# Merged stores and paired reads in a five-stage macaron block, with half-precision projections and fewer token buffers

## The chip, the cores and the metric

The kernel runs on one core of a Trainium2 chip. The metric is device time in microseconds (us) of one execution, and a kernel's figure is the median of several executions. Profile views come from one further execution that was profiled.

Engine names: PE is TensorE (PEld its weight loads), DVE is VectorE, ACT is ScalarE, POOL is GpSimd, SP is SyncE, which here only issues transfers. A trailing q (SPq, ACTq) means the sequencer of that engine, for instance while it issues a DMA. L134 is line 134 of the kernel.

## The reference

The input is `x` of 8 sequences by 1024 tokens by 256 channels. Three residual blocks follow one another:

```python
x = x + 0.5 * ffn(layernorm(x))
x = x + attn(layernorm(x))
x = x + 0.5 * ffn(layernorm(x))        # the same weights as the first

def ffn(x):                            # x_prev: the token before, zero at the start
    xr = mu_r * x + (1 - mu_r) * x_prev
    xk = mu_k * x + (1 - mu_k) * x_prev
    return sigmoid(xr @ W_r.T) * (square(relu(xk @ W_k.T)) @ W_v.T)

def attn(x):                           # 16 heads of 16; 40 offsets o: 0..32, 48, 64, 96, 128, 192, 256, 384
    q, k, v = split(x @ qkv_w.T + qkv_b)
    logit[o] = (q[n] . k[n-o]) / 4 * (1 + q[n] . scale_embed[o]) + pos_bias[o]   # masked where n < o
    out = sum_o softmax(logit)[o] * v[n-o] * if_gain
    return (out * sigmoid(x @ gate_w.T + gate_b)) @ out_w.T + out_b
```

Every query therefore looks at 33 near keys ("local") and 7 far ones.

## The kernel before

A *chunk* is 256 tokens (32 of them), a *tile* is 128 tokens (64 of them), a *half* is 512 tokens of a sequence (16 of them, index `i`; `hf` says first or second half). Five generators each do their part of the work step by step:

- `stage_f1`, the first FFN, one chunk per step. Its `load` reads a chunk into `x1[c]` (L220), from a pool `px1` of 13 buffers. A buffer lives until `stage_f2` has stored the chunk (L229).
- `stage_p`, the projections, one chunk per step. The normalised and transposed input is split into `xh` and the remainder `xl`, both float32r, and the weights likewise into `wa_hi` and `wa_lo`. `proj` sums three products (high by high, high by low, low by high), 12 matmuls for each of q, k and the gate, and 12 more for v. For q and for k, and for each half `g` of the channels, ACT writes the float16 value and DVE the float16 remainder into a tile `hl` (L263, L264, four buffers). Two transfers then write that tile to DRAM in two arrangements (L270), since q is needed as high, low, high, low and k as high, high, low, low.
- `stage_qk`, the scores, four steps per half. It reads q (`qst`, L317) and k (`kb`, L319) back from DRAM, and computes far scores and then local scores of 128 queries at a time. `scores` fills a PSUM bank per `g`, ACT copies it into a tile `sl` (L308, two buffers), and four transfers of 32 partitions each store the tile: far scores at L346, local scores at L362. In the first half of a sequence there are two tiles of far scores, in the second half four; local scores always take four tiles.
- `stage_att`, the attention, one tile per step. It loads the tile's local scores along the diagonals (`lg`, L377, three buffers), the far scores (`ef`, L379, two buffers), the local values (`vw`, L385, two transfers into one of two tiles) and the values at distance 32, 48 and 64 (`v3`, L391, L395). Scaling by `1 + q.scale_embed` is L405 and L410, the softmax L419 to L430. The local probabilities are stored (L426, on ACT's queue) and read back into `pd` (L428, one buffer) so that PE can transpose them (L464) and multiply them with `vw` (L473). Every second tile the output projection is added to `x1` (L505).
- `stage_f2`, the second FFN, one chunk per step, and the store of the result.

`norm_transposed` writes two tiles `xn` (L160) per chunk, which PE transposes into one PSUM bank (L162). The stages run in lanes: `stage_f1` has the lane "a", `stage_f2` mostly "b", `stage_p` mostly "p", and each lane has its own PSUM bank (tag `"ps" + s`) and its own two `xn` buffers (tag `"xn" + s`).

The order of the work is fixed at compile time. The steps are sorted by their place plus an offset from `TRACE`; each runs under a priority of its place plus an offset from `RANK`, and the framework's scheduler, which has a timing model, turns the priorities into one order per engine. Each engine, and the queue of each issuing engine, executes that order strictly.

```python
TRACE = (0, 3.6, -4.4, -8.1, -10.6)      # att, f2, qk, p, f1
RANK = (0, 5.1, -4.4, -8.1, -10.6)
for k, kind, stage in sorted(steps, key=lambda s: (s[0] + TRACE[s[1]], s[1])):
    with tc.high_priority(-int(1000 * (k + RANK[kind] + 20))):
        next(stage)
```

`k` counts tiles. Other pools that bound how far a stage may run ahead are `pga` (five gates), `pvn` (six chunks of values) and `pq` (four q tiles).

Of the kernel before, what the change touches and what calls it, by code (L numbers as in the profile page):

```python
# [8 lines left out]
F32 = mybir.dt.float32  # L9
F32R = mybir.dt.float32r  # L10
# [29 lines left out]
F2A = 28  # L40
TRACE = (0, 3.6, -4.4, -8.1, -10.6)
# [8 lines left out]
def macaron(ctx: ExitStack, tc: tile.TileContext, x, wffn, watt, wo, cols, rows, pbias, se, mask, out):  # L50
# [16 lines left out]
    wa_hi = const.tile([128, 4, 2, 256], F32R, name="wa_hi")  # L67
    wa_lo = const.tile([128, 4, 2, 256], F32R, name="wa_lo")
# [4 lines left out]
    vw = [const.tile([128, 4, 2, 8, 17], F32, name=f"vw{i}") for i in range(2)]  # L73
# [7 lines left out]
    px1 = pool("px1", 13)  # L81
# [11 lines left out]
    def load_att():  # L93
        with tc.tile_pool(name="setup", bufs=1) as sp:
            wst = sp.tile([128, 4, 2, 256], F32, name="wst")
            nc.sync.dma_start(wst, watt.rearrange("w (c p) d -> p w c d", p=128))
            nc.vector.tensor_scalar(wst[:, 0], wst[:, 0], 0.25, None, ALU.mult)
            nc.vector.tensor_copy(wa_hi, wst)
            nc.vector.tensor_tensor(wa_lo, wst, wa_hi.bitcast(F32), ALU.subtract)
            nc.vector.tensor_scalar(b_q, b_q, 0.25, None, ALU.mult)  # L100
            nc.vector.tensor_scalar(b_g, b_g, 0.5, None, ALU.mult)
            nc.sync.dma_start(row, rows.unsqueeze(0).to_broadcast([128, 2, 256]))
            for t in [t.bitcast(F32) for t in kb] + vw:
                nc.gpsimd.memset(t, 0.0)
            zero = kb[1].bitcast(F32).rearrange("p a b w -> p (a b w)")
            for i in range(2):
                nc.sync.dma_start(v_d[i][0 : VPAD * VROW].rearrange("(p w) -> p w", p=VPAD), zero[:VPAD, :VROW])
            nc.sync.dma_start(sf_d[0:PADF].rearrange("(p w) -> p w", p=16), zero[:16, : PADF // 16])
            for c0, c1, w in ((0, 8, 384), (8, 15, 384), (15, 16, 368)):
                o = PADF + c0 * ROW + ROW - 384  # L110
                nc.sync.dma_start(flat(sf_d, o, (SF_T, 32), (ROW, c1 - c0), (1, w)), zero[:32, : (c1 - c0) * w])
            nc.sync.dma_start(flat(pd_d, NL * 16, (4 * SKEW, 128), (SKEW, 4), (1, SKEW - NL * 16)), zero[:, : 4 * 512])
            nc.sync.dma_start(bias, pbias.to_broadcast([128, NO * 16]))
            nc.sync.dma_start(msk, mask.rearrange("t p u -> p t u"))
            nc.sync.dma_start(wot, wo.rearrange("(c p) d -> p c d", p=128))
            for c in range(2):
                nc.vector.tensor_scalar(wot[:, c], wot[:, c], gain[:, c : c + 1], 0.5, ALU.mult, ALU.mult)
            se_f = sp.tile([128, NO], F32, name="se_f")
            se_h = sp.tile([128, NO], F16, name="se_h")
            for h2 in range(2):  # L120
                nc.sync.dma_start(se_f[64 * h2 : 64 * h2 + 64], se.unsqueeze(1).to_broadcast([16, 4, NO]))
            nc.vector.memset(seb, 0.0)
            nc.vector.tensor_scalar(se_f, se_f, 4.0, None, ALU.mult)
            nc.vector.tensor_copy(se_h, se_f)
            nc.vector.tensor_tensor(se_f, se_f, se_h, ALU.subtract)
            nc.vector.tensor_scalar(se_f, se_f, slot[:, 1:2], None, ALU.mult)
            for h2 in range(2):
                a = slice(64 * h2, 64 * h2 + 64)
                nc.vector.scalar_tensor_tensor(seb[a, h2], se_h[a], slot[a, 0:1], se_f[a], ALU.mult, ALU.add)
# [25 lines left out]
    def norm_transposed(x2, y, nb, k0, s):  # L155
        tr = ps.tile([128, 2, 256], F32, name="tr", tag="ps" + s)
        for i in range(2):
            k = k0 + i
            xn = pw.tile([128, 256], F32, name="xn", tag="xn" + s, bufs=2)
            nc.scalar.activation(xn, x2[:, i], AF.Identity, bias=nb[:, k : k + 1], scale=y[:, k : k + 1])  # L160
            for c in range(2):
                nc.tensor.transpose(tr[:, c, i * 128 : i * 128 + 128], xn[:, c * 128 : c * 128 + 128], ident)  # L162
        return tr
# [69 lines left out]
    def stage_p():  # L233
        for c in range(NCH):
# [7 lines left out]
            xh = pw.tile([128, 2, 256], F32R, name="xh", tag="xk" + s)  # L242
            xl = pw.tile([128, 2, 256], F32R, name="xl", tag="xr" + s)
            nc.scalar.copy(xh, tr)
            nc.vector.tensor_tensor(xl, tr, xh.bitcast(F32), ALU.subtract)
# [13 lines left out]
            for j, bb in ((0, b_q), (1, b_k)):  # L259
                p = proj(j)  # L260
                for g in range(2):
                    hl = pw.tile([128, 2, 256], F16, name="hl", bufs=4)
                    nc.scalar.activation(hl[:, 0], p[:, g], AF.Identity, bias=bb[:, g : g + 1])  # L263
                    nc.vector.scalar_tensor_tensor(  # L264
                        hl[:, 1], p[:, g], bb[:, g : g + 1], hl[:, 0], ALU.add, ALU.subtract
                    )
                    o = g * 128 * 2048 + cq * 256
                    for r in range(2):
                        ro, s2 = (r * 1024, 512) if j == 0 else (r * 512, 1024)
                        nc.sync.dma_start(flat(qk_d[i % 2][j], o + ro, (2048, 128), (s2, 2), (1, 256)), hl)  # L270
            p = proj(3)
            for g in range(2):
                nc.scalar.activation(gt[:, g], p[:, g], AF.Tanh, bias=b_g[:, g : g + 1], scale=0.5)
# [23 lines left out]
    def stage_qk():  # L297
        def scores(o, g, q4, q, k, keys):
# [9 lines left out]
            nc.scalar.copy(o[:, :, :, g], p.rearrange("n (q h j) -> n j h q", q=4, h=2))  # L308

        for i in range(2 * B):  # L310
# [14 lines left out]
            for th in range(nth):  # L325
                sf = psb.tile([128, 64, 2, 2, 4], F32, name="sl")
                for g in range(2):
                    scores(
                        sf,
                        g,  # L330
                        lambda a: [slice(c, 512, 16) for c in range((4 * th + a) * ns, (4 * th + a + 1) * ns)],
                        qs[i, g],
                        kb[g],
                        lambda ms: slice(LW + ms.start, LW + (hf + 1) * 512, 16),
                    )
                for a in range(4):
                    c = (4 * th + a) * ns
                    o = PADF + hf * 32 * SF_T + c * ROW
                    src = sf[32 * a : 32 * a + 32].rearrange("n j h g q -> n (j h g q)")
                    if hf == 0:  # L340
                        dst = flat(far, o, (SF_T, 32), (ROW, 2), (1, 512))
                        src = src.rearrange("n (s w) -> n s w", s=2)
                    else:
                        w = ROW - 16 if c == 15 else ROW
                        dst, src = flat(far, o, (SF_T, 32), (1, w)), src[:, :w]
                    nc.sync.dma_start(dst, src)  # L346
                if 2 * th + 2 == nth:
                    yield
            yield
            for t in range(4):  # L350
                sl = psb.tile([128, 64, 2, 2, 4], F32, name="sl")
                for g in range(2):
                    scores(
                        sl,
# [5 lines left out]
                    )  # L360
                for a in range(4):
                    nc.sync.dma_start(  # L362
                        flat(sl_d[i % 2], (4 * t + a) * BLK, (ROW, 32), (1, ROW)),
                        sl[32 * a : 32 * a + 32].rearrange("n j h g q -> n (j h g q)"),
                    )
                if t % 2:
                    yield

    def stage_att():
        for tt in range(B * NT):  # L370
# [3 lines left out]
            lg = pat.tile([128, NO, 16], F32, name="lg", bufs=3)  # L374
            ll = lg[:, 0:NL].rearrange("p u e -> p (u e)")
            lf = lg[:, NL:]
            nc.sync.dma_start(ll, flat(sl_d[i % 2], 4 * t4 * BLK, (SKEW, 128), (1, NL * 16)))  # L377
            ef = pat.tile([128, FW, 16], F32, name="ef")
            nc.sync.dma_start(  # L379
                ef.rearrange("p u e -> p (u e)"),  # L380
                flat(sf_d, PADF - 384 + t * 128 * ROW, (ROW, 128), (1, FW * 16)),
            )
            vwt = vw[tt % 2]
            for h2 in range(2):
                nc.sync.dma_start(  # L385
                    vwt[h2::2, :, h2].rearrange("p q a w -> p q (a w)"),
                    flat(v_d[b % 2], (VPAD - LW + t * 128) * VROW + h2 * 136, (VROW, 64), (32 * VROW, 4), (1, 136)),
                )
            v3 = v3s[tt] = pv1.tile([128, 3, 16, 17], F32, name="v3")
# [7 lines left out]
            )  # L397
            for h2 in range(2):
                gp = ps.tile([128, 64, 8], F32, name="gp")
                for g in range(2):  # L400
# [5 lines left out]
                    lg[:, 0:NL, e], gp[:, 0:NL], 1.0, lg[:, 0:NL, e], ALU.add, ALU.mult  # L406
                )
                for k0, k1 in FARG:
# [4 lines left out]
                        1.0,  # L413
# [172 lines left out]
```

## Time and profile before

| what | us |
|---|---|
| median of 3 executions | 1260.52 (1255.84 to 1267.22) |
| the profiled execution | 1256.76 |
| its span, first to last instruction | 1254.0 |
| PE busy | 1089.2 (87%) |
| DVE busy | 942.6 (75%) |
| POOL busy | 766.5 (61%) |
| ACT busy | 538.0 (43%) |

The granted TensorE clock was 0.956 of full speed. DMA moved 282.88 MB. Busy time counts each engine's own instructions as a union of their spans; for PE it includes the pipelined ends of matmuls, so it is more than the array's own time. The *chain of waits* is the chain of work that ended last, followed back from the last instruction to whatever released each step. A group row gives line, engine, operation, tiles written and read, shapes, count, then busy us and mean ns, then idle time before the group and what ended it. A row of DMA issues gives KB per transfer and the median us from issue to landing.

### The profile page before, as it was taken

The page shows a single profiled execution, that of the slowest core. Times are in us where ns is not written, and L with a number is a line of the kernel's source. Part 1 is how long each engine was busy: PE and PEld are TensorE (multiplying, and loading weights), DVE is VectorE, ACT ScalarE, POOL GpSimd, SP SyncE. Part 2 cuts the span into 40 slices and gives each one's busy share as a digit, 9 for nine tenths or more (in the row PEclk, how much of TensorE's full clock was granted, in tenths as well). Part 3 has the DMA queues.
Part 4 walks back from the last instruction along what each step waited for, and adds up shares of the span by engine and source line. Part 5 has one row for each costly group of instructions (what it writes and reads, how often), then busy time and mean ns, then how long its engine had stood idle before and what let it go on. Part 6 is the DMA issues. An engine that isn't in the chain of part 4 may idle for free.

```text
span 1254.0 us, 34712 instructions
## 1 busy us (share of the span) xinstructions
PE 1089.2 (87%) x13568; PEld 885.7 (71%) x13568; DVE 942.6 (75%) x2266; ACT 538.0 (43%) x1025; POOL 766.5 (61%) x1101
## 2 busy tenths in 40 slices
PE   2887989899799898989899989899988998888785
PEld 2676768677687677777777778786777787665664
DVE  7546768987587888879678866978858887877772
ACT  2444445344453444536345454544534444524231
POOL 7436619675575656659457564867656755657672
PEclk9999999899999999899999999999989999998988
DMA  8187888786878779787788977797787868998630
GB/s 263 32 224 222 241 242 265 229 238 194 251 226 254 230 233 274 221 252 232 193 260 257 254 201 230 228 269 227 233 243 234 269 197 254 284 280 265 202 99 24
DMA packets 256500, 282.88 MB, mean 226 GB/s; under 512 B 23440, under 2 KB 214608, under 8 KB 256336
## 3 DMA queue, kind: packets, MB, share of 16 engines
q1 hardware_dynamic: 247120, 263.36, 71.7%
q10 hardware_dynamic: 9216, 17.31, 3.8%
q8 instruction: 106, 1.74, 0.6%
q14 instruction: 58, 0.48, 0.1%
HBM read 151.67 MB, written 128.91 MB: 224 GB/s over the span
## 4 chain that ended last, share of the span: by engine, by line
PE 42%; DMA 25%; DVE 14%; SPq 6%; POOL 5%; issue 5%; ACT 4%; POOLq 0%; ACTq 0%; DVEq 0%
PE p L134 29%; DMA pd<-pd 9%; PE tra L464 4%; PE pv L134 3%; PE tra L134 3%; POOL prod L445 2%; DMA lg<-sl 2%; DMA x<-in_x_dram 2%; DMA qk<-hl 2%; DMA kb<-qk 2%; DMA sl<-sl 2%; DVE prod L457 2%; DVE xk L196 1%; PE gp L134 1%; DVE mx L423 1%
## 5 line engine op out<-in xcount | busy, mean ns | idle before, releaser
L134 PEld LDWEIGHTS <-qst 128*32 128x32 f16 (+1 forms) x5120 | 157.2, 120 | 100.1 <-issue 63.5
L134 PE MATMUL p<-kb,qst 128*32 128x128 f16 (+1 forms) x4096 | 185.1, 297 | 12.7 <-ACT sl L308 8.6
L308 ACT COPY sl<-p 128x512 f32<-128x512 f32 x224 | 130.8, 584 | 144.2 <-PE p L134 123.0
L445 POOL TENSOR_TENSOR prod<-v,lg 128x256 f32<-128x256 f32 x248 | 165.5, 687 | 10.2 <-ACT lg L425 6.1
L134 PE MATMUL p<-xk,w_f 128*128 128x256 f32 x512 | 144.9, 421 | 20.0 <-DVE xk L196 11.7
L419 POOL TENSOR_TENSOR lg<-lg,bias 128x640 f32<-128x640 f32 x64 | 113.5, 1774 | 71.8 <-DVE lg L410 66.9
L213 POOL TENSOR_TENSOR x<-x,xr 128x512 f32<-128x512 f32 x64 | 88.4, 1382 | 109.0 <-DVE xr L212 94.9
L457 DVE TENSOR_TENSOR prod<-prod 128x512 f32<-128x512 f32 (+2 forms) x120 | 126.1, 1051 | 32.1 <-POOL prod L445 31.5
L464 PE MATMUL tra<-ident,pd 128*128 128x128 f32 x512 | 97.1, 313 | 58.3 <-DMA pd<-pd 54.9
L160 ACT ACTIVATE xn<-x,nb,y 128x256 f32<-128x256 f32 x192 | 110.8, 602 | 63.0 <-DVE nb L152 55.2
L134 PE MATMUL p<-w_f,xk 128*128 128x256 f32 x512 | 132.9, 400 | 1.7 <-ACT xr L206 1.3
L134 PE MATMUL p<-w_f,xr 128*128 128x256 f32 x512 | 130.4, 396 | 3.6 <-ACT xk L201 2.8
L445 POOL TENSOR_TENSOR prod<-vn,lg 128x256 f32<-128x256 f32 x144 | 96.0, 678 | 54.3 <-ACT lg L425 35.4
L134 PE MATMUL p<-xh,wa_hi 128*128 128x256 f32 x384 | 123.2, 321 | 5.6 <-DVE hl L264 4.4
L134 PEld LDWEIGHTS p<-xk,w_f 128*128 128x128 f32 x512 | 99.3, 208 | 39.8 <-issue 10.5
L470 ACT COPY ptt<-tra 128x512 f32<-128x512 f32 x128 | 74.9, 585 | 116.1 <-PE tra L464 113.0
L464 PEld LDWEIGHTS tra<-ident,pd 128*128 128x128 f32 x512 | 71.0, 197 | 73.9 <-DMA pd<-pd 68.0
L263 ACT ACTIVATE hl<-p,col 128x256 f16<-128x256 f32 x128 | 60.6, 474 | 121.1 <-PE p L134 68.6
L134 PE MATMUL p<-xh,wa_lo 128*128 128x256 f32 x384 | 111.5, 290 | 0.0
L134 PE MATMUL p<-xl,wa_hi 128*128 128x256 f32 x384 | 111.4, 290 | 0.0
L134 PEld LDWEIGHTS p<-w_f,xr 128*128 128x128 f32 x512 | 95.3, 196 | 19.4 <-ACT xk L201 5.8
L134 PEld LDWEIGHTS p<-w_f,xk 128*128 128x128 f32 x512 | 96.0, 198 | 15.9 <-issue 2.8
(82 smaller groups left out, 2394.2 us busy)
## 6 DMA issues: line engine op xcount, KB each, us to landing
qk<-hl SPq DMA_DIRECT2D x256, 128.0 KB, 3.4
sl<-sl SPq DMA_DIRECT2D x256, 128.0 KB, 3.8
pd<-pd SPq DMA_DIRECT2D x64, 512.0 KB, 4.8
sf<-sl SPq DMA_DIRECT2D x184, 128.0 KB, 3.1
vw<-vd SPq DMA_DIRECT2D x128, 136.0 KB, 4.1
v<-vd SPq DMA_DIRECT2D x64, 272.0 KB, 4.3
lg<-sl SPq DMA_DIRECT2D x64, 264.0 KB, 4.1
pd<-lg ACTq DMA_DIRECT2D x64, 264.0 KB, 3.8
```

What stands on the lines that cost most here:

```text
L134: nc.tensor.matmul(o, l, r, start=start, stop=stop)
L160: nc.scalar.activation(xn, x2[:, i], AF.Identity, bias=nb[:, k : k + 1], scale=y[:, k : k + 1])
L196: nc.vector.scalar_tensor_tensor(o[:, h], xr[:, h], mu[:, h : h + 1], prev[:, h], ALU.mult, ALU.add)
L213: nc.gpsimd.tensor_tensor(x2, x2, xr, ALU.add)
L263: nc.scalar.activation(hl[:, 0], p[:, g], AF.Identity, bias=bb[:, g : g + 1])
L308: nc.scalar.copy(o[:, :, :, g], p.rearrange("n (q h j) -> n j h q", q=4, h=2))
L419: nc.gpsimd.tensor_tensor(la, la, bias, ALU.add)
L423: nc.vector.tensor_reduce(mx, lg.rearrange("p u e -> p e u"), AX.X, ALU.max)
L445: nc.gpsimd.tensor_tensor(prod[:, k], shifted[k][1]()[:, :, 0:16], lf[:, k].unsqueeze(2).to_broadcast([128, 16, 16]), ALU.mult,)
L457: nc.vector.tensor_tensor(o, terms[:, 0:m], terms[:, n - m : n], ALU.add)
L464: nc.tensor.transpose(tr[:, pr * 128 : pr * 128 + 128], pd.rearrange("p (m e) -> p m e", e=8)[:, :, 4 * g + pr], ident,)
L470: nc.scalar.copy(ptt.rearrange("p q n -> p (q n)"), tr)
```

## The change

1. The projections use float16 for `xh`, `xl`, `wa_hi` and `wa_lo` instead of float32r. Weights and biases are scaled by 16 (`WS`), and later operations take the factor out again.
2. `hl` is `[128, 2, 2, 256]`: ACT and DVE read the PSUM result through a broadcast and write it twice, in the arrangement that DRAM wants, and one transfer stores it. There are two such buffers instead of four.
3. `sl` holds two tiles of scores (still two buffers), and each group of 32 partitions is stored once for both. In the first half of a sequence both far tiles fall into one step and the next step is empty.
4. `lg`, `ef` and `vw` hold two tiles; they are read at every even tile. `lg` has two buffers of two tiles instead of three of one, `ef` one of two tiles instead of two of one, `vw` two of two tiles instead of two of one.
5. `px1` has 10 buffers instead of 13, and all lanes share three `xn` buffers instead of having two each.

```diff
-    wa_hi = const.tile([128, 4, 2, 256], F32R, name="wa_hi")
-    wa_lo = const.tile([128, 4, 2, 256], F32R, name="wa_lo")
+    wa_hi = const.tile([128, 4, 2, 256], F16, name="wa_hi")
+    wa_lo = const.tile([128, 4, 2, 256], F16, name="wa_lo")
...
-    vw = [const.tile([128, 4, 2, 8, 17], F32, name=f"vw{i}") for i in range(2)]
+    vw = [const.tile([128, 8, 2, 8, 17], F32, name=f"vw{i}") for i in range(2)]
...
-    px1 = pool("px1", 13)
+    px1 = pool("px1", 10)
...
-            xn = pw.tile([128, 256], F32, name="xn", tag="xn" + s, bufs=2)
+            xn = pw.tile([128, 256], F32, name="xn", bufs=3)
...
-            xh = pw.tile([128, 2, 256], F32R, name="xh", tag="xk" + s)
-            xl = pw.tile([128, 2, 256], F32R, name="xl", tag="xr" + s)
+            xh = pw.tile([128, 2, 256], F16, name="xh", tag="xh" + s)
+            xl = pw.tile([128, 2, 256], F16, name="xl", tag="xl" + s)
...
-                    hl = pw.tile([128, 2, 256], F16, name="hl", bufs=4)
-                    nc.scalar.activation(hl[:, 0], p[:, g], AF.Identity, bias=bb[:, g : g + 1])
-                    nc.vector.scalar_tensor_tensor(
-                        hl[:, 1], p[:, g], bb[:, g : g + 1], hl[:, 0], ALU.add, ALU.subtract
-                    )
-                    o = g * 128 * 2048 + cq * 256
-                    for r in range(2):
-                        ro, s2 = (r * 1024, 512) if j == 0 else (r * 512, 1024)
-                        nc.sync.dma_start(flat(qk_d[i % 2][j], o + ro, (2048, 128), (s2, 2), (1, 256)), hl)
+                    hl = pw.tile([128, 2, 2, 256], F16, name="hl", bufs=2)
+                    hi, lo = (hl[:, :, 0], hl[:, :, 1]) if j == 0 else (hl[:, 0], hl[:, 1])
+                    pp = p[:, g : g + 1].to_broadcast([128, 2, 256])
+                    nc.scalar.activation(hi, pp, AF.Identity, bias=bb[:, g : g + 1])
+                    nc.vector.scalar_tensor_tensor(lo, pp, bb[:, g : g + 1], hi, ALU.add, ALU.subtract)
+                    nc.sync.dma_start(
+                        flat(qk_d[i % 2][j], g * 128 * 2048 + cq * 256, (2048, 128), (512, 4), (1, 256)),
+                        hl.rearrange("p a b n -> p (a b) n"),
+                    )
...
-                sf = psb.tile([128, 64, 2, 2, 4], F32, name="sl")
+                if th % 2 == 0:
+                    sf = psb.tile([128, 2, 64, 2, 2, 4], F32, name="sl")
...
+                if th % 2 == 0:
+                    continue
...
-                if 2 * th + 2 == nth:
+                if hf and th == 1:
                     yield
+            if not hf:
+                yield
             yield
...
-                    nc.sync.dma_start(
-                        flat(sl_d[i % 2], (4 * t + a) * BLK, (ROW, 32), (1, ROW)),
-                        sl[32 * a : 32 * a + 32].rearrange("n j h g q -> n (j h g q)"),
-                    )
+                        flat(sl_d[i % 2], (4 * (t - 1) + a) * BLK, (ROW, 32), (4 * BLK, 2), (1, ROW)),
+                        sl[32 * a : 32 * a + 32].rearrange("n t j h g q -> n t (j h g q)"),
+                    )
...
-            lg = pat.tile([128, NO, 16], F32, name="lg", bufs=3)
...
-            ef = pat.tile([128, FW, 16], F32, name="ef")
...
-            vwt = vw[tt % 2]
...
+            if j == 0:
+                lg2 = pat.tile([128, 2, NO, 16], F32, name="lg")
...
+                ef2 = pat.tile([128, 2, FW, 16], F32, name="ef", bufs=1)
...
+                vw2 = vw[tt // 2 % 2]
...
+            lg, ef, vwt = lg2[:, j], ef2[:, j], vw2[:, 4 * j : 4 * j + 4]
```

## The prediction

> **What bounds the kernel now.** I read busy shares first, then the chain of waits, then the SP queue's own waits, then the timeline of the matmuls that change type.
>
> ```profile
> PE 1089.2 (87%) x13568; PEld 885.7 (71%) x13568; DVE 942.6 (75%) x2266; ACT 538.0 (43%) x1025; POOL 766.5 (61%) x1101
> ...
> DMA  8187888786878779787788977797787868998630
> ...
> q1 hardware_dynamic: 247120, 263.36, 71.7%
> ...
> PE 42%; DMA 25%; DVE 14%; SPq 6%; POOL 5%; issue 5%; ACT 4%; POOLq 0%; ACTq 0%; DVEq 0%
> ```
>
> No engine is full. PE's 87% overstates it, because matmuls overlap: gaps between matmul starts of at most 300 ns sum to 904 us, 72% of the span. DVE is 75% busy and the 16 DMA engines 76% (q1, q10 and the small queues). The chain changes hands all the time: 42% PE, 25% a transfer's flight, 14% DVE, 6% SP issuing. So this is five interleaved stages in an order fixed at compile time, and it loses time where an in-order queue stands before something not ready. An edit is worth what it does to those meetings, not the busy time it removes.
>
> ```profile
> SPq L377 <- DMA sl<-sl: 47.1, 54, 3.7
> ...
> SPq L346 <- ACT sl L308: 30.0, 21, 5.3
> ...
> SPq L270 <- DVE hl L264: 24.1, 18, 6.0
> ```
>
> SP issues every transfer but the probability stores. The durations of its 1,360 DMA instructions sum to 736 us (59% of the span); gaps over 200 ns between them, where it stands on a semaphore (rows above: us, times, longest), sum to 447 us. It is almost always occupied, yet only 6% of the chain runs through its issuing.
>
> **The change part by part.** I sum against the profiled execution, 1256.76 us (span 1254.0).
>
> *Half-precision projections* (1,536 matmuls). Mean durations mislead here, so take starts:
>
> ```profile
> 602.80 0.28 PE L134 MATMUL p<-xl,wa_hi 128*128 128x256 f32 x1
> 602.92 0.28 PE L134 MATMUL p<-xh,wa_lo 128*128 128x256 f32 x1
> 603.04 0.28 PE L134 MATMUL p<-xh,wa_hi 128*128 128x256 f32 x1
> ```
>
> Each lasts 0.28 us but the next starts 0.12 us later. The float32 matmuls of the same 256 columns show 216 ns for a record of two passes, so 108 ns for one. Half precision can save 120 - 108 = 12 ns each, 18 us of PE time, not 1,536 x (290 - 110) = 276 us. PE holds 42% of the chain: **-9 us**. The setup's few longer operations and twice the zeroing of vw (1.0 us each) cost **+3**.
>
> *Merged transfers: issuing.* q/k stores go from 256 to 128 instructions, near scores 256 to 128, far scores 192 to 96, value reads 128 to 64, lg and ef reads 64 to 32 each: 480 fewer on SP. Lines L270, L362, L385, L379, L346 and L377 hold 14.1 + 11.6 + 7.7 + 5.2 + 4.5 + 3.0 = 46 us of the chain as SP issue. Half as many, each somewhat longer (0.42 us for a score store, 0.61 for the k read with more dimensions), leaves about 26: **-20**. The Trainium skill's "DMA: Bandwidth & Descriptors", section "Issuing engines are not separate DMA queues", speaks against the edit: issue time is usually small beside the transfer. By it this term is near 0; here issue is 0.4 to 0.6 us beside flights of 3.1 to 4.1, and the chain shows it, so I keep -20.
>
> *Merged transfers: flight.* Bytes and packets stay (q/k remain 65,536 packets of 512 B).
>
> ```profile
> qk<-hl SPq DMA_DIRECT2D x256, 128.0 KB, 3.4
> sl<-sl SPq DMA_DIRECT2D x256, 128.0 KB, 3.8
> ...
> lg<-sl SPq DMA_DIRECT2D x64, 264.0 KB, 4.1
> ...
> kb<-qk SPq DMA_DIRECT2D x64, 256.0 KB, 5.1
> ```
>
> The same page's section "Anatomy of one DMA" fits 2.0 us + bytes/436 GB/s (for another issuing path): doubling 128 KB would move 2.3 to 2.6 us, +13%. The rows say 3.1 to 3.8 becomes 4.5 to 5.1 at 256 KB (x 4.5, kb 5.1), about +40%. The four kinds that double (qk, sl, sf, vw) hold 21.2 + 20.8 + 16.1 + 12.3 = 70 us of the chain: +9 by the rule, +28 by the rows; I take **+18**. In return an odd tile no longer waits for its own scores: lg<-sl holds 27.7 us of the chain; half goes, a later landing takes some back: **-10**.
>
> *The probability round trip.* Its reload (L428) is issued on average 4.2 us, median 2.5, after its store landed, behind other SP work; pd<-pd holds 115 us of the chain. It is untouched, but stands in a shorter queue: between 0 and -20; I take **-8**, because much of the delay is the single pd buffer's (13.4 us of SP wait on PE tra).
>
> *q/k tiles of double width.* ACT and DVE now write 512 elements per partition.
>
> ```profile
> L264 DVE SCALAR_TENSOR_TENSOR hl<-p,col,hl 128x256 f16<-128x256 f32 x128 | 60.3, 472 | 24.7 <-ACT hl L263 24.4
> L201 ACT ACTIVATE xk<-p 128x512 f32<-128x512 f32 x64 | 38.1, 595 | 74.7 <-PE p L134 69.1 <-POOL t L149 2.9 <-issue 2.1
> L245 DVE TENSOR_TENSOR xl<-tr,xh 128x512 fp32r<-128x512 f32 x32 | 21.8, 681 | 9.3 <-ACT xh L244 9.1
> ```
>
> By the 512-wide rows DVE goes 472 to 680 ns (+27 us, to 77% busy), ACT 474 to 595 (+15). Bounds: 14% of 27, +4, and all 27. The chain's own hl pieces (14.6 and 5.3 us) scaled by these ratios give **+8**.
>
> *Two hl buffers instead of four.* Now a buffer has landed 18 us or more before its reuse (lowest twentieth). At distance two, k's halves would want q's buffers: in the trace as it stands 21 of 64 come before that landing, by 20 us in sum, and the median margin is 1.3 us. A 256 KB store lands some 1.2 us later (+1.7 flight, -0.5 for one issue less): about half of the 64 then wait, some 1.5 us each, 48 us on ACT's in-order queue. Behind such a wait stand the score and ptt copies, which PE's banks wait for. Between 0 and 48; a quarter, since ACT has 57% slack: **+12**.
>
> *Three xn buffers for all lanes instead of two for each of three.* Matching each xn with its transposes: the second transpose ends a median 21 us after xn was written, because the lane's only PSUM bank is still held by its previous chunk. More than three are alive for 690 us of the span; 84 of 189 are written before the third-last is free. So this prefetch is used, and a lane far from its turn can hold buffers another lane needs. Each such pair exposes two ACT passes and transposes, 1.6 us: 42 x 1.6 = 67. Between 0 and 67; a quarter, as for hl: **+16**.
>
> *Ten token buffers instead of thirteen.* Every load after the 13th is issued 3 to 24 us after the store that frees its buffer; 13 chunks live each time. Chunk 21's load, issued at 553, would have to wait for chunk 11's store, at 638. Its pair ran the first FFN from 578 to 659; stage p on it started at 676, and five gate buffers hold p's end to attention of chunk 15, at 716. That leaves 78 us for what took 81: no stop, but the lead is gone, and a load is needed as it lands. x loads and st hold 24 + 12 us of the chain; a third more is **+12** (bounds 0 and 36).
>
> *One answer each.* ef with one pair buffer has most of a 20 us tile to refill; lg and vw become two pairs, no shorter a lead. Both far passes of a first half go into one step and leave the next empty; attention comes two or more steps later, 0.
>
> **Sum:** gains 9 + 20 + 10 + 8 = 47, costs 3 + 18 + 8 + 12 + 16 + 12 = 69, net +22: 1279 on the profiled execution, 1282 on the median 1260.52. I predict **1280 us**, slower by 1.6%; about 1% is what a measurement here can tell from none.
>
> **Rivals.**
> - *SP is the bottleneck* (faster, 0.33). For it: 59% issuing, 36% waiting, 480 instructions gone, pd's lag. Against: 6% of the chain. All of pd's 20 us goes and recompiled order absorbs lost prefetch: -9 - 20 - 10 - 20 + 3 + 18 + 8 = -30: **1229**. It decides if L428's mean lag falls below about 2.5 us.
> - *Lanes couple through xn* (slower, part of my side, 0.12). Hl and xn cost near two thirds of their bounds: (48 + 67) x 2/3 = 77 instead of 28: **1328**. It decides once ACT's wait at L160 on transposes, now 6.9 us, passes some 40 us.
> - *Traffic bounds it* (0.17). DMA share is 0.80 to 0.82 between 150 and 1100 us, and bytes do not change: **1258**. Against: single slices reach 284 GB/s where the mean is 226.
>
> **How the numbers follow.** Modest loss 0.38, lane coupling 0.12, no change 0.17, faster 0.33: slower 0.50, same 0.17, faster 0.33. The forecast's own range is 1264 to 1300. With all cover gone the costs reach 3 + 28 + 27 + 48 + 67 + 36 = 209, unlikely together; with rivals, 1205 to 1328 leaves about 2 in 10 outside.
>
> **What would show it.** Right: SP issue near 500 us yet span not shorter; wider hl near 600 and 680 ns; ACT waiting at hl or xn on a transfer or transposes; projection starts at 0.11 us; doubled stores landing in 4.5 to 5 us. Wrong: pd<-pd well under 115 us in the chain with ACT's waits unchanged (the SP rival), or DMA share rising with span falling.

## The result and the profile after

The changed kernel takes 1389.14 us (median of 4 executions, 1386.56 to 1394.18) beside 1260.23 us before (median of 4, one more than in the table above): a ratio of 1.102, 95% interval 1.096 to 1.108. Slower was forecast, but 1280 us: the forecast's own range ended at 1300 us, and with its rivals at 1328.

The page of the changed kernel, busy times, the main DMA queue and the chain by engine:

```profile
PE 1103.8 (80%) x13568; PEld 852.4 (62%) x13568; DVE 966.2 (70%) x2268; ACT 572.2 (41%) x1026; POOL 765.5 (55%) x1101
...
DMA  7278786785786677776687756898576785798630
...
q1 hardware_dynamic: 239440, 263.09, 66.2%
...
PE 28%; DMA 28%; DVE 23%; POOL 8%; issue 4%; ACT 4%; SPq 4%; ACTq 0%; POOLq 0%; DVEq 0%
```

The work is nearly the same: DVE has 24 us more, ACT 34, PE 15. The span grew by 131 us. No engine became the bottleneck; each engine stands idle for longer. PE's share of the chain fell by 14 points and DVE's rose by 9. Inside the chain, by tile, the transfers that lead from the projections to the scores grew most: qk<-hl from 21 to 75 us and kb<-qk from 21 to 64, while pd<-pd fell from 115 to 77. The granted clock is 0.912 instead of 0.956, but the three groups of FFN matmuls are busy for 409.5 us in all, against 408.2 before, so the lower clock does not show in the length of these matmuls.

Waits of the changed kernel (us in total, times, longest us), and below them the same of the kernel before:

```profile
POOL x L217 <- DVE xr L216: 169.1, 43, 11.1
...
PE gp L138 <- DVE lg L428: 54.9, 38, 7.7
...
PE p L138 <- DMA kb<-qk: 41.6, 19, 6.8
...
ACT hl L270 <- DMA qk<-hl: 25.3, 12, 3.7
```

```profile
POOL x L213 <- DVE xr L212: 94.9, 29, 9.5
...
PE p L134 <- DMA kb<-qk: 1.6, 1, 1.6
```

POOL idles before the FFN's residual addition, and hands the residual on later. Two waits are new, or nearly so: PE stands before scores whose keys have not been read back, and ACT before an `hl` buffer whose store has not landed (no such row before).

The SP queue's own waits in the changed kernel:

```profile
SPq L272 <- DVE hl L271: 90.8, 41, 27.9
SPq L406 <- POOL prod L463: 80.4, 35, 9.4
...
SPq L324 <- DMA qk<-hl: 51.5, 22, 5.0
SPq L322 <- DMA qk<-hl: 39.4, 21, 5.3
...
SPq L224 <- DMA out_dram<-x: 24.8, 15, 3.3
```

and two rows of the kernel before:

```profile
SPq L317 <- DMA qk<-hl: 25.2, 21, 4.2
...
SPq L319 <- DMA qk<-hl: 4.0, 7, 2.3
```

SP issues for 579 us instead of 736; its gaps of over 200 ns sum to 767 us instead of 447. The freed queue time turned into waiting for data: the reads of q and k (L322, L324) wait 91 us for the projections' stores, where the two rows held 29 us before. The last of the changed kernel's rows is the token ring: a load behind the store that frees its buffer. The timeline of SP shows store and load in pairs, the load for a chunk ten later than the one stored:

```profile
660.28 0.40 SPq L233 DMA_DIRECT2D out_dram<-x  x1
664.04 0.38 SPq L224 DMA_DIRECT2D x<-in_x_dram  x1
685.07 0.38 SPq L233 DMA_DIRECT2D out_dram<-x  x1
688.76 0.37 SPq L224 DMA_DIRECT2D x<-in_x_dram  x1
```

The smaller steps, by groups, by issues (KB each, us to landing) and by the PE timeline of the changed kernel:

```profile
L270 ACT ACTIVATE hl<-p,col 128x512 f16<-128x512 f32 x128 | 87.9, 686 | 157.6 <-PE p L138 71.7
...
L271 DVE SCALAR_TENSOR_TENSOR hl<-p,col,hl 128x512 f16<-128x512 f32 x128 | 94.7, 740 | 51.0 <-ACT hl L270 50.9
...
qk<-hl SPq DMA_DIRECT2D x128, 256.0 KB, 4.3
sl<-sl SPq DMA_DIRECT2D x128, 256.0 KB, 4.5
...
lg<-sl SPq DMA_DIRECT2D x32, 528.0 KB, 5.4
```

```profile
509.92 0.27 PE L138 MATMUL p<-xl,wa_hi 128*128 128x256 f16 x1
510.03 0.27 PE L138 MATMUL p<-xh,wa_lo 128*128 128x256 f16 x1
510.14 0.27 PE L138 MATMUL p<-xh,wa_hi 128*128 128x256 f16 x1
```

### The profile page after: what moved, and what is told of

Its sections match the earlier page's. It is cut to its first block, busy times and chain, and to the rows that moved or that the text cites. A ratio compares the mean times of both kernels' runs of the same rounds, so it can differ in the third digit from the quotient of the medians.

```text
span 1384.8 us, 33990 instructions
## 1 busy us (share of the span) xinstructions
PE 1103.8 (80%) x13568; PEld 852.4 (62%) x13568; DVE 966.2 (70%) x2268; ACT 572.2 (41%) x1026; POOL 765.5 (55%) x1101
## 4 chain that ended last, share of the span: by engine, by line
PE 28%; DMA 28%; DVE 23%; POOL 8%; issue 4%; ACT 4%; SPq 4%; ACTq 0%; POOLq 0%; DVEq 0%
PE p L138 19%; DMA pd<-pd 6%; DMA qk<-hl 5%; DMA kb<-qk 5%; POOL prod L463 3%; DMA lg<-sl 3%; DMA x<-in_x_dram 3%; DVE prod L475 3%; DVE xk L200 3%; PE tra L482 3%; DMA sl<-sl 2%; PE pv L138 2%; DVE mx L441 2%; PE tra L138 2%; DMA out_dram<-x 2%
## 5 line engine op out<-in xcount | busy, mean ns | idle before, releaser
L138 PE MATMUL p<-kb,qst 128*32 128x128 f16 (+1 forms) x4096 | 176.9, 293 | 52.9 <-DMA kb<-qk 41.6
L313 ACT ACTIVATE sl<-p 128x512 f32<-128x512 f32 x224 | 133.4, 596 | 151.3 <-PE p L138 143.7
L270 ACT ACTIVATE hl<-p,col 128x512 f16<-128x512 f32 x128 | 87.9, 686 | 157.6 <-PE p L138 71.7
L271 DVE SCALAR_TENSOR_TENSOR hl<-p,col,hl 128x512 f16<-128x512 f32 x128 | 94.7, 740 | 51.0 <-ACT hl L270 50.9
L475 DVE TENSOR_TENSOR prod<-prod 128x512 f32<-128x512 f32 (+2 forms) x120 | 118.8, 990 | 16.2 <-POOL prod L463 15.6
L138 PE MATMUL p<-xh,wa_hi 128*128 128x256 f16 x384 | 109.8, 286 | 24.3 <-DVE hl L271 14.4
L211 POOL TENSOR_TENSOR xk<-xk 128x512 f32<-128x512 f32 x64 | 69.7, 1089 | 85.5 <-ACT xk L205 85.4
L138 PE MATMUL gp<-seb,qst 128*128 128x40 f16 x1024 | 68.5, 218 | 59.9 <-DVE lg L428 54.9
L423 DVE SCALAR_TENSOR_TENSOR lg<-gp,lg 128x264 f32<-128x264 f32 x128 | 54.2, 424 | 86.4 <-PE gp L138 44.0
L138 PEld LDWEIGHTS pv<-vw,ptt 128*32 128x32 f32 x4096 | 87.4, 153 | 42.7 <-issue 23.3
```

What stands on the lines that cost most here:

```text
L138: nc.tensor.matmul(o, l, r, start=start, stop=stop)
L211: nc.gpsimd.tensor_tensor(xk, xk, xk, ALU.mult)
L270: nc.scalar.activation(hi, pp, AF.Identity, bias=bb[:, g : g + 1])
L271: nc.vector.scalar_tensor_tensor(lo, pp, bb[:, g : g + 1], hi, ALU.add, ALU.subtract)
L313: nc.scalar.mul(o[:, :, :, g], p.rearrange("n (q h j) -> n j h q", q=4, h=2), WS**-3)
L475: nc.vector.tensor_tensor(o, terms[:, 0:m], terms[:, n - m : n], ALU.add)
```

## The experiments

Each kernel is compared with the kernel before on its own chip; ratios carry 95% intervals. Three readings come from each trace. *Projection lead*: median over chunks 10 to 25 of the time from the start of the last POOL operation of `stage_p` on a chunk (L294 before) to that of attention's residual (L505 before). *FFN lead*: the same from the first FFN's residual addition on POOL (L213 before), which is told from the second FFN's by the store that follows the latter. *Kept order*: of 191 neighbouring `xn` writes on ACT, how many go against the order in which the program creates the tiles; the rows don't name the chunk, so these counts are less sure than the other readings.

| kernel | parts of the change in it | token buffers | xn buffers | ratio | projection lead, us | FFN lead, us | PE waits on kb, us |
|---|---|---|---|---|---|---|---|
| before | none | 13 | 2 each lane | 1 | 224 | 277 | 1.6 |
| b_f16 | half precision | 13 | 2 each | 0.999 (0.996 to 1.001) | 227 | 272 | none |
| f_more | half precision | 15 | 3 each | 1.003 (1.001 to 1.006) | 224 | 270 | 12.3 |
| f_hl | + q/k stores | 13 | 2 each | 1.006 (1.003 to 1.009) | 222 | 308 | 18.8 |
| f_scores | + score stores | 13 | 2 each | 1.019 (1.014 to 1.024) | 234 | 292 | 10.8 |
| a_stores | + both stores | 13 | 2 each | 1.010 (1.005 to 1.015) | 228 | 297 | 15.1 |
| f_reads_px12 | + paired reads | 12 | 2 each | 1.012 (1.006 to 1.017) | 235 | 266 | 12.1 |
| b_px10 | none | 10 | 2 each | 1.046 (1.041 to 1.052) | 199 | 236 | 22.7 |
| b_xn3 | none | 13 | 3 shared | 1.061 (1.055 to 1.068) | 180 | 230 | 45.3 |
| b_px10_xn3 | none | 10 | 3 shared | 1.065 (1.057 to 1.072) | 177 | 223 | 30.3 |
| b_xn1_each | none | 13 | 1 each | 1.007 (1.004 to 1.009) | 188 | 277 | 19.5 |
| b_xn6_shared | none | 13 | 6 shared | 1.105 (1.098 to 1.112) | 196 | 240 | 48.2 |
| n_px10_xn6 | both stores | 10 | 2 each | 1.076 (1.072 to 1.080) | 212 | 248 | 30.8 |
| n_px13_xn3 | both stores | 13 | 3 shared | 1.107 (1.102 to 1.112) | 188 | 241 | 35.1 |
| n_px13_xn1 | both stores | 13 | 1 each | 1.060 (1.053 to 1.068) | 185 | 323 | 39.0 |
| a_noreads | both stores | 10 | 3 shared | 1.088 (1.082 to 1.093) | 187 | 232 | 37.4 |
| a_vw1_px13_xn1 | stores, lg and ef pairs | 13 | 1 each | 1.055 (1.050 to 1.060) | 188 | 326 | 41.2 |
| a_vw1_ef2 | same, two ef pair buffers | 13 | 1 each | 1.041 (1.035 to 1.047) | 195 | 313 | 23.7 |
| a_xn1_each | all | 10 | 1 each | 1.102 (1.097 to 1.108) | 186 | 244 | 21.6 |
| changed | all | 10 | 3 shared | 1.102 (1.096 to 1.108) | 181 | 234 | 41.6 |

All kernels at or below 1.02 but one have a projection lead of 222 us or more and a wait of PE on kb below 20 us; all above 1.04 have less lead, at most 212 us, and more of that wait. The one apart is b_xn1_each, with 188 us and 1.007. What sets it apart is its FFN lead: that is 277 us, as before, and its first FFN still runs a median 10 chunks ahead of the second.

In every kernel with ten token buffers or a shared `xn` pool the first FFN is only 8 chunks ahead (median over its chunks 8 to 25), the FFN lead is 223 to 248 us, and the kernel is at least 4.6% slower. The three kernels with merged stores, thirteen token buffers and one `xn` buffer for each lane lose 4 to 6% although the first FFN stays 10 or 11 chunks ahead: there its chunks wait longer for the projections (the two leads lie 118 to 138 us apart, 53 before). None of these readings ranks the losses (a_xn1_each has half the wait on kb of the changed kernel, and the same time), so they show where work comes late, not how many us each lead is worth. Differences of one or two points between two versions should not be read as the cost of one edit either: f_scores came out slower than a_stores, which contains it.

### One buffer count at a time in the kernel before

**b_px10**

```diff
-    px1 = pool("px1", 13)
+    px1 = pool("px1", 10)
```

> The kernel before with ten token buffers instead of thirteen, nothing else. Theory R (the ring of token buffers: a load waits for the store ten chunks earlier, so the first FFN, the projections and the scores all come late): 1320 to 1390 us, with x loads and q/k transfers in the chain. Theory X (three xn buffers for all lanes couple the lanes): 1250 to 1275. Theory M (the merged transfers and the wider q/k tiles themselves): 1250 to 1275.

Measured 1.046, 1329.89 us. Theory R holds in size. The FFN lead falls from 277 to 236 us, and a chunk's life from load to store from 475 to 388 us: ten chunks at 38.8 us instead of thirteen at 36.5. In the chain x<-in_x_dram, qk<-hl and kb<-qk together rise from 5.3% to 9.2%. Keys come late to PE, but SP's reads of q and k wait no longer than before (29.8 us in all, against 29.2), so that wait of the changed kernel comes from elsewhere:

```profile
PE p L134 <- DMA kb<-qk: 22.7, 10, 4.1
...
SPq L317 <- DMA qk<-hl: 21.9, 20, 3.4
...
SPq L319 <- DMA qk<-hl: 7.9, 8, 2.1
```

**b_xn3**

```diff
-            xn = pw.tile([128, 256], F32, name="xn", tag="xn" + s, bufs=2)
+            xn = pw.tile([128, 256], F32, name="xn", bufs=3)
```

> The kernel before with three xn buffers shared by all lanes instead of two for each, nothing else. Theory X: 1320 to 1390 us, with the transposes of L162 and xn in the chain. Theory R: 1255 to 1280. Theory M: 1255 to 1280.

Measured 1.061, 1345.67 us. Theory X holds in size, beside R, not instead of it. It didn't hold in place: ACT's idle time at L160 for transposes is 3.7 us, less than the 6.9 before. So the lanes don't stand and wait for one another's buffers at run time; the compiled order itself is a different one. The two FFNs' residual additions on POOL show it most plainly: after eight of the first FFN they alternate strictly, one of each, until the first FFN is done. That is the order of the program, where the offsets in `TRACE` put the second FFN 14.2 tiles, or 7.1 chunks, behind the first. In the kernel before, eleven of the first FFN come before the second's first.

**b_px10_xn3** has both edits.

> The kernel before with ten token buffers and three shared xn buffers, transfers as before. The first cost 4.6% alone and the second 6.1%. If they are separate losses they multiply: 1.110, near 1400 us. If both take the same thing, the lead of the first FFN and the projections over attention (277 us from the first FFN's result to attention before, 236 and 230 in the two single runs), the sum is little more than the larger: 1.06 to 1.08, 1340 to 1370 us, and the lead stays near 230.

Measured 1.065, 1354.24 us: the two take the same thing, and after either the other adds little (1.046 to 1.065, 1.061 to 1.065). The FFN lead is 223 us. One thing that they have in common can be read off: each alone brings the first FFN from 10 chunks ahead to 8, and both together leave it at 8.

### Is it the number of xn buffers or their being shared?

**b_xn1_each** and **b_xn6_shared**

```diff
-            xn = pw.tile([128, 256], F32, name="xn", tag="xn" + s, bufs=2)
+            xn = pw.tile([128, 256], F32, name="xn", tag="xn" + s, bufs=1)   # b_xn1_each
+            xn = pw.tile([128, 256], F32, name="xn", bufs=6)                # b_xn6_shared
```

> The kernel before with one xn buffer for each of the three lanes: three in all, as in the change, but not shared. Theory of sharing (a lane far from its turn holds what another needs): 1255 to 1290 us. Theory of number (the prefetch itself is what is missed): 1330 to 1370, as with three shared.

> The kernel before with six xn buffers in one pool for all lanes: as many as before, but shared. Theory of sharing: 1300 us or more. Theory of number: 1255 to 1275.

Measured 1.007 with three buffers that are not shared, 1.105 with six that are. It is the sharing; the number alone costs 0.7% here, although ACT then does wait for transposes:

```profile
ACT xn L160 <- PE tr L162: 35.0, 20, 6.5
```

The order on ACT tells why. In the kernel before, 27 of 191 neighbouring `xn` writes go against the program's order of creation (60 in b_xn1_each): a lane whose data is ready writes ahead of a step that stands earlier in the program. In all six kernels with a shared pool that were run (b_xn3, b_xn6_shared, b_px10_xn3, n_px13_xn3, a_noreads and the changed one) it is 0 of 191. With a shared pool the lanes normalise in the program's order, and in all six the two FFNs' residual additions alternate strictly after the first eight, as in b_xn3. In b_xn6_shared they also come in bursts. ACT's timeline there:

```profile
533.76 1.09 ACT L160 ACTIVATE xn<-x,nb,y 128x256 f32<-128x256 f32 x2
...
543.09 0.61 ACT L160 ACTIVATE xn<-x,nb,y 128x256 f32<-128x256 f32 x1
628.50 3.07 ACT L160 ACTIVATE xn<-x,nb,y 128x256 f32<-128x256 f32 x6
633.04 0.62 ACT L160 ACTIVATE xn<-x,nb,y 128x256 f32<-128x256 f32 x1
```

and of the kernel before:

```profile
494.75 0.59 ACT L160 ACTIVATE xn<-x,nb,y 128x256 f32<-128x256 f32 x1
507.96 0.59 ACT L160 ACTIVATE xn<-x,nb,y 128x256 f32<-128x256 f32 x1
...
529.22 1.08 ACT L160 ACTIVATE xn<-x,nb,y 128x256 f32<-128x256 f32 x2
554.27 0.60 ACT L160 ACTIVATE xn<-x,nb,y 128x256 f32<-128x256 f32 x1
557.00 0.61 ACT L160 ACTIVATE xn<-x,nb,y 128x256 f32<-128x256 f32 x1
578.07 1.09 ACT L160 ACTIVATE xn<-x,nb,y 128x256 f32<-128x256 f32 x2 [0.63 <-DVE nb L152]
```

In the first, twelve tiles are written within 11 us and then none for 85 us; in the second the writes lie spread. The bursts are not what all shared pools have in common: between 150 and 1100 us the longest pause is 94 us in b_xn6_shared, but 63 in b_xn3 and 59 in the kernel before. Why six shared buffers cost more than three is not settled; larger bursts fit the trace, but no run parts that from another order.

### The parts that were meant to gain

**b_f16** (half precision and its scaling alone)

```diff
-            xh = pw.tile([128, 2, 256], F32R, name="xh", tag="xk" + s)
-            xl = pw.tile([128, 2, 256], F32R, name="xl", tag="xr" + s)
+            xh = pw.tile([128, 2, 256], F16, name="xh", tag="xh" + s)
+            xl = pw.tile([128, 2, 256], F16, name="xl", tag="xl" + s)
...
-    wa_hi = const.tile([128, 4, 2, 256], F32R, name="wa_hi")
+    wa_hi = const.tile([128, 4, 2, 256], F16, name="wa_hi")
```

> The kernel before with the half-precision projections alone (weights scaled by 16), every buffer count and transfer as before. All theories: 1235 to 1265 us; a projection matmul starts about 0.11 us after the last instead of 0.12. If a new compiled order alone can cost several per cent, this run shows it.

Measured 0.999 (1269.11 us beside 1269.79 on that chip): nothing. A new compiled order alone did not cost several per cent here.

**f_scores**, b_f16 with the score part of the change alone:

```diff
-                sl = psb.tile([128, 64, 2, 2, 4], F32, name="sl")
+                if t % 2 == 0:
+                    sl = psb.tile([128, 2, 64, 2, 2, 4], F32, name="sl")
```

> Half-precision projections and the merged stores of scores alone, all buffer counts of the kernel before, two transfers for each q and k tile, single reads. If the issuing of transfers on SP bounds the kernel: 1225 to 1250 us. If it doesn't, and the wider q/k tiles are what made the version with both stores 1.0% slower: 1255 to 1275.

Measured 1.019, above what either theory allowed. It takes 224 instructions off SP and is slower. Which of its two parts, far or local, costs was not run.

**f_hl**, b_f16 with the q/k part alone:

```diff
-                    hl = pw.tile([128, 2, 256], F16, name="hl", bufs=4)
+                    hl = pw.tile([128, 2, 2, 256], F16, name="hl", bufs=2)
```

> Half-precision projections and the wide q/k tiles with one store each, two hl buffers, alone; score stores, reads and all other buffers as before. By the difference between both stores merged (1.010) and score stores alone (1.019), 0.985 to 0.998: 1248 to 1266 us. By the prediction's cost of the wide tiles and of two hl buffers: 1.01 to 1.02.

Measured 1.006: between the two expectations, so the 1.0% and 1.9% of the other two versions don't simply subtract. The wait that was feared is there, 20 us in 9 waits:

```profile
ACT hl L270 <- DMA qk<-hl: 19.5, 9, 4.2
```

**a_stores**, the changed kernel with single reads, whose room goes to full buffers:

```diff
-    px1 = pool("px1", 10)
+    px1 = pool("px1", 13)
...
-            xn = pw.tile([128, 256], F32, name="xn", bufs=3)
+            xn = pw.tile([128, 256], F32, name="xn", tag="xn" + s, bufs=2)
...
-                lg2 = pat.tile([128, 2, NO, 16], F32, name="lg")
+            lg = pat.tile([128, NO, 16], F32, name="lg", bufs=3)
```

> The changed kernel with reads of one tile as before (which frees the room), thirteen token buffers and two xn buffers for each lane; the merged stores of q, k and scores and the half-precision projections stay. Theories R and X: 1220 to 1275 us, all or nearly all of the loss gone. Theory M, if the stores and the hl tiles are the cause: 1340 to 1390; if the paired reads are: 1220 to 1275, so this run alone parts the stores from the rest.

Measured 1.010, 1283.67 us, a little above the range: with its buffers back and single reads, the kernel with merged stores is within about 1% of the kernel before. Merging the stores alone neither gains nor does the damage.

**f_reads_px12**, b_f16 with paired reads:

```diff
-    px1 = pool("px1", 13)
+    px1 = pool("px1", 12)
...
-            lg = pat.tile([128, NO, 16], F32, name="lg", bufs=3)
+                lg2 = pat.tile([128, 2, NO, 16], F32, name="lg")
```

> Half-precision projections and the paired reads of lg, ef and vw alone, with twelve token buffers (thirteen don't fit), two xn buffers for each lane, stores as before. By the difference of the changed kernel with and without them (1.102 against 1.088) the paired reads cost about 1.4%: 1265 to 1300 us. If SP bounds the kernel: 1230 to 1255.

Measured 1.012, no gain either (one token buffer fewer is part of it).

**f_more**, b_f16 with `px1` at 15 and three `xn` buffers for each lane.

> Half-precision projections, with the room they free spent on fifteen token buffers and three xn buffers for each lane. If the lead of the first FFN still bounds the kernel before at thirteen: 1235 to 1258 us. If thirteen is past the point where it matters: 1258 to 1275, no change.

Measured 1.003: no gain, so thirteen and two each are enough. A chunk then lives 552 us from load to store, 15 at 36.8 us: the extra buffers only let loads come earlier.

### Which cut holds the loss once the stores are merged?

**a_noreads**: the changed kernel with the reads of one tile, buffers as in the change.

> The changed kernel with reads of one tile as before (lg, ef and vw single), ten token buffers and three shared xn buffers kept. If the paired reads cost nothing: 1370 to 1400 us, as the changed kernel. If they hold a part of the 10%: 1330 to 1365. If they help: over 1400.

Measured 1.088, 1378.69 us. In us that lies where the reads were to cost nothing; by the ratios, each on its own chip, the paired reads add 1.4 points to the change; f_reads_px12, with 1.2% alone, points the same way.

**a_xn1_each**

```diff
-            xn = pw.tile([128, 256], F32, name="xn", bufs=3)
+            xn = pw.tile([128, 256], F32, name="xn", tag="xn" + s, bufs=1)
```

> The changed kernel with one xn buffer for each lane instead of three shared: the same memory, everything else of the change kept. Theory of order (a shared pool hands its buffers out in the program's order, so that no lane may normalise ahead of a step that stands before it): the xn part of the loss goes and what remains is the ten token buffers (4.6% alone), the stores (1.0%) and the paired reads (about 1.4%): 1.05 to 1.075, 1330 to 1365 us, and the order of xn writes leaves the program's order again. If the token buffers alone already took the same lead, little is won: 1375 to 1395 us.

Measured 1.102, as the changed kernel. 59 of 191 writes leave the program's order again, the first FFN stays 8 chunks ahead, and nothing is won. The expectation built from single losses fell.

**n_px10_xn6** and **n_px13_xn3**: a_noreads with one of the two cuts undone.

```diff
-            xn = pw.tile([128, 256], F32, name="xn", bufs=3)
+            xn = pw.tile([128, 256], F32, name="xn", tag="xn" + s, bufs=2)   # n_px10_xn6
...
-    px1 = pool("px1", 10)
+    px1 = pool("px1", 13)                                                    # n_px13_xn3
```

> The changed kernel with single reads, ten token buffers kept and two xn buffers for each lane (with both reduced it was 1.088, with both restored 1.010). If the token buffers hold the loss and the merged stores make their ring dearer than the 4.6% they cost alone: 1.07 to 1.09, 1355 to 1385 us. If the two are alike and not additive: 1.05 to 1.065.

> The changed kernel with single reads, three shared xn buffers kept and thirteen token buffers. If the order of the shared pool costs here what it cost alone (6.1%): 1.06 to 1.08. If the token ring is what counts once the stores are merged: 1.01 to 1.03.

Measured 1.076 and 1.107, the second above both of its ranges. Either cut is enough, and undoing one saves at most 1.2 points. With the shared pool, three more token buffers even cost 1.9 points, and the first FFN is no further ahead: the order holds it at 8 chunks, whatever the ring has room for. The ring of ten costs 6.5% beside merged stores (1.076 over 1.010) where it cost 4.6% alone. The shared pool costs 9.6% with thirteen token buffers (1.107 over 1.010), more than with ten.

**n_px13_xn1**: a_noreads with `px1` at 13 and one `xn` buffer for each lane.

> The changed kernel with all reads single, thirteen token buffers and one xn buffer for each lane. If the paired lg and ef reads hold the 4.5%: 1.01 to 1.025, as with two xn buffers for each lane. If one xn buffer is too few beside the merged stores (alone it cost 0.7%): 1.04 to 1.06.

Measured 1.060. One `xn` buffer for each lane, which cost 0.7% alone, costs 4.9% beside the merged stores (1.060 over 1.010). The projection lead is nearly the same in both (188 and 185 us), but ACT's wait on the `hl` store differs. It has no such row in b_xn1_each; in n_px13_xn1:

```profile
PE p L138 <- DMA kb<-qk: 39.0, 17, 4.9
ACT hl L270 <- DMA qk<-hl: 37.9, 17, 4.5
```

**a_vw1_px13_xn1** and **a_vw1_ef2**: the changed kernel with single value reads, 13 token buffers and one `xn` buffer for each lane; the second also

```diff
-                ef2 = pat.tile([128, 2, FW, 16], F32, name="ef", bufs=1)
+                ef2 = pat.tile([128, 2, FW, 16], F32, name="ef", bufs=2)
```

> The changed kernel with single reads of the local values (their room goes to thirteen token buffers) and one xn buffer for each lane; paired reads of lg and ef and all merged stores stay. If the token buffers are what the room was taken from to no good: 1.01 to 1.035, 1280 to 1310 us. If the paired reads or the ef buffer hold the loss that a_xn1_each kept: 1.06 to 1.10.

> The version with single value reads, thirteen token buffers, one xn buffer for each lane and paired lg and ef, now with two ef pair buffers instead of one. If the wait for ef's only pair buffer holds the 4.5%: 1.01 to 1.03. If not: 1.045 to 1.065.

Measured 1.055 and 1.041, each between its two ranges, so neither expectation holds. The first is not slower than n_px13_xn1 (1.060), which has no paired reads: so the pairs of `lg` and `ef` don't hold the loss, the single `xn` buffer beside merged stores does. A second `ef` buffer gives 1.3%.

No version beats the kernel before.

## Why the prediction was wrong in size

Direction and kind were right: no engine fills, SP's queue is relieved, and what that is traded for costs more. That the direction came out is partly luck, since the sum set 47 us of gains, of which the runs found none, against costs that it took too small. The steps that failed are the two buffer terms, 12 and 16 us, and their joining with the rest: the two cuts alone make the kernel before 6.5% slower (b_px10_xn3), about 81 us instead of 28. All other terms summed to -6 us; the rest of the loss, some 48 us, is what half precision, merged stores and paired reads cost beside those cuts, where alone none of them cost more than 2%.

- **Ten token buffers, +12 us.** Measured alone 4.6%, about 58 us, above the prediction's upper bound of 36. The step saw the lead vanish ("no stop, but the lead is gone") and then priced only the x loads' own pieces of the chain. The lost lead shows elsewhere: the first FFN 8 chunks ahead instead of 10, keys that reach PE too late (a wait of 22.7 us instead of 1.6), POOL waiting 154 us for the FFN's result instead of 95.
- **Three xn buffers, +16 us of at most 67.** Measured alone 6.1%, about 77 us. The step took the cut for one of number and priced exposed passes and transposes for 42 pairs of tiles. b_xn1_each shows that number at 0.7%. What costs in the kernel before is the one argument removed, `tag="xn" + s`: without it the first FFN no longer runs ahead of the program's order. Beside the merged stores the number costs too (4.9%), and in the changed kernel itself, with ten token buffers, giving each lane its own buffer wins nothing (a_xn1_each). The rival that lanes couple through xn named the right place, but looked for a wait of ACT at L160 on transposes; that wait stayed at 7.1 us (6.9 before), below the 40 us that should have decided. In b_xn1_each the same wait rose to 35.0 us and the kernel lost 0.7%, so it was the wrong sign to look for.
- **A quarter of each bound, and a sum.** The quarter had no row behind it. And the terms don't add: the cuts overlap with each other (1.046 and 1.061 give 1.065), and each is dearer beside the merged stores (one xn buffer each: 0.7% alone, 4.9% there). In steps from the kernel before: both stores 1.010, ten token buffers 1.076, shared xn 1.088, paired reads 1.102. By another path the shares differ (1.010, shared xn 1.107, ten token buffers 1.088, paired reads 1.102), so no share is a cut's own. Why merged stores make the cuts dearer stays open. The waits that come with them are known: the projections' stores then hold ACT (`hl`, two buffers) and the reads of q and k. But they don't follow the loss: ACT's wait is 19 us in a_noreads (1.088) and 43 us in a_vw1_px13_xn1 (1.055).
- **Issuing on SP, -20 us.** SP issues 157 us less, but no run with merged transfers is faster: f_scores +1.9%, f_hl +0.6%, f_reads_px12 +1.2%. SP's own gaps grew by more than its issuing fell (320 us against 157). The counter-argument that the prediction set aside, that this term is near 0, held. The SP rival is out, although pd<-pd fell to 77 us of the chain, which was to speak for it: ACT's waits had changed, and the reload came later, not sooner. The -10 for odd tiles' scores is out too: DVE's wait on lg<-sl is 36.8 us against 33.6.
- **The probability round trip, -8 us.** Its reload's mean lag behind the landed store rose from 4.2 to 5.7 us.
- **Half precision, -9 us.** The spacing of 0.11 us came out, the time did not: b_f16's interval allows a gain of 5 us at most. (42% of 18 us is 8, not 9.)
- **Near enough:** the doubled stores land in 4.3 and 4.5 us (4.5 to 5.1 estimated from rows), about a fifth to a quarter later than before. The wide `hl` operations are longer than the rows taken: ACT 686 ns, not 595, and DVE 740, not 680. The two `hl` buffers' wait on ACT, taken at 48 us before the quarter, is 25 us in the changed kernel and between 17 and 50 us in the other versions with these tiles.
- **The traffic rival** is out: between 150 and 1200 us the DMA share fell to between 0.69 and 0.75, while the bytes stayed.

## What to carry to other kernels

In this software pipeline, in which no engine is full, the buffers that let an early stage run ahead were worth more than a third of SP's transfer instructions; measure how long before its use each stage's result stands ready, and by how many chunks one stage leads another, and suspect any cut that shortens either. Before two lanes are given one pool, compare the compiled order with and without it: three private buffers cost 0.7% here, six shared ones 10.5%. Costs found one at a time don't add: try the cut together with the change that is to pay for it.

## What had not been expected of the hardware

Nothing in the engines' or queues' own durations, but two sizes: ACT takes 686 ns for a float16 result of 512 elements read from PSUM through a broadcast, where a float32 result of that size takes 595 ns without one, and DVE 740 where 681 was the nearest row. And the granted TensorE clock is lower in the slow kernels (0.956 before, 0.946 in b_xn1_each, 0.926 in b_px10, 0.912 in the changed one, 0.896 in n_px13_xn3), while the mean of the p<-xk,w_f matmuls stays at 420 to 421 ns before and after. It does not follow the time alone: b_f16 takes as long as the kernel before with 0.938. What sets it was not studied.
